# Powers on GpSimd in place of square roots and reciprocals, and forced placement of some scan products, in a two-layer image network

## The chip, the cores and the metric

The kernel runs on one core of a Trainium2 chip. The metric is the device time in microseconds (us); the time before is the median of three runs. A core has five engines, which the profile calls PE (TensorE, matmul), DVE (VectorE), ACT (ScalarE), POOL (GpSimd) and SP (SyncE, which here only issues DMAs). Each engine takes its own instructions in the order of its queue.

## The reference

Sixteen images of 48 x 48 pixels with 96 channels pass through two layers. Each layer has a convolution block with a selective scan and then a small feed-forward network, each behind a layer norm. What matters here:

```python
def _ln_c(v, eps=1e-6):              # _ln_t is the same with eps=1e-5
    m = jnp.mean(v, axis=-1, keepdims=True)
    s = jnp.var(v, axis=-1, keepdims=True)
    return (v - m) / jnp.sqrt(s + eps)
...
def step(h, inp):                    # four directions k, 192 channels d, 16 states n
    d_t, u_t, B_t, C_t = inp
    h = h * jnp.exp(d_t[..., None] * A) + (d_t * u_t)[..., None] * B_t[:, :, None, :]
    return (h, jnp.einsum('bkdn,bkn->bkd', h, C_t))
...
x = x + _L0_conv_ref(_ln_c(x), ...)
t = t + _L0_ffn_ref(_ln_t(t), ...)
x = x + _L1_conv_ref(_ln_c(x), ...)  # has a norm over 192 channels of its own, rsqrt(var + 1e-05)
t = t + _L1_ffn_ref(_ln_t(t), ...)
```

So an image has five norms, 80 in all, each with one square root per pixel. The convolution blocks also use silu, softplus and sigmoid.

## The kernel before

An image and a layer make a phase, 32 phases in all. A phase is 288 scan steps, each on tiles of 128 partitions x 768 pixels; 128 partitions are 32 channels times 4 states. `scans` (L559) writes the order of all instructions out by hand: for each step n it first lets a piece of the other work run, then issues the step.

A scan step n consists of:

- the decay a = exp(rate * d), by ScalarE into PSUM (`decays`, L611). It is issued two steps ahead, and there are two such buffers.
- the product b = (delta * u) * B, by GpSimd (`added`, L617), issued three steps ahead; there are four b buffers, and one comes free when the scan that reads it is done.
- the scan h = a * h + b along the pixels, by VectorE (`step`, L674)
- the product hc = h * C, by VectorE or by GpSimd (L678). `here` (L670) decides which: two running sums, `load["gp"]` and `load["ve"]`, hold the time booked so far for GpSimd and VectorE, and a product goes to the one that is behind. If VectorE takes it, it follows its scan at once and h stays in PSUM, in a's place. If GpSimd takes it, h goes to SBUF, and the product stands behind b of step n+3 in GpSimd's queue.
- a copy of the last column into `carry` by ScalarE (L684), where the scan goes on in the next chunk
- matmuls by TensorE that sum hc over the states (`folded`, L641)

The other work of a phase is a set of generators (`first`, `middle`, `final`, L1020 to L1047) that prepare the next phase's inputs and finish those of the last one. Each `yield` gives a weight; a phase gives out the weights evenly between its steps 6 and 276. What they book for VectorE and GpSimd with `ve` and `gp` enters the two running sums. In this work stand the operations that the change touches:

- `norm` (L334), 64 times: a mean and a centring, squares by ScalarE (L350), their sum s by VectorE (L353), `Sqrt` by ScalarE (L356), `reciprocal` by VectorE (L359), and 18 scaled activations by ScalarE (L362)
- `centred` (L893), 16 times: sums by TensorE into PSUM (L920), `Sqrt` by ScalarE (L931), `reciprocal` by VectorE (L933)
- `Silu` at L468, L492 and L774, `Softplus` at L551 and `Sigmoid` at L842, by ScalarE, which are in other tables than the scan's `Exp`

Of the kernel before, what the change touches and what calls it, by code (L numbers as in the profile page):

```python
# [13 lines left out]
F32 = mybir.dt.float32  # L14
F16 = mybir.dt.float16
F8 = mybir.dt.float8e5
AF = mybir.ActivationFunctionType
ALU = mybir.AluOpType
# [5 lines left out]
DM = 96  # L24
DI = 192
NS = 16
DR = 6
NT = L // 128
# [9 lines left out]
SPARE = 1.0  # L38
# [99 lines left out]
class Net:  # L138
    def __init__(self, ctx, tc, wpack, at, b2, ffw):
        self.tc, self.nc = tc, tc.nc  # L140
        nc = self.nc
# [31 lines left out]
            nc.vector.tensor_tensor(c, c, self.ident[n, n], ALU.add)  # L173
        self.ident16 = self.const.tile([128, 128], F16, name="ident16")
        nc.vector.tensor_copy(self.ident16, self.ident)
        self.ones16 = self.const.tile([128, 128], F16, name="ones16")
        nc.vector.memset(self.ones16, 0.0)
        nc.vector.memset(self.ones16[:1, :], 1.0)
# [84 lines left out]
            self.taps[name] = d  # L263


        self.load = {"gp": 0.0, "ve": 0.0}


        self.s = []
# [59 lines left out]
    def ve(self, us):  # L329
        self.load["ve"] += us  # L330

    def norm(self, x, eps):  # L334

        nc = self.nc
        m = self.small.tile([128, NT], F32, name="m")
        nc.vector.tensor_reduce(m, x, AX.X, ALU.add)  # L338
        nc.vector.tensor_scalar_mul(m, m, -1.0 / DM)
        self.ve(2.4)  # L340
        yield 1
        xm = self.bigt([128, NT, DM], "xm")
        for i in range(NT):
            nc.scalar.activation(xm[:, i, :], x[:, i, :], AF.Identity, bias=m[:, i : i + 1])  # L344
            if i % 3 == 2:
                yield 0.8
        sq = self.bigt([128, NT, DM], "sq")
        for i in range(2):
            at = slice(i * NT // 2, (i + 1) * NT // 2)
            nc.scalar.activation(sq[:, at], xm[:, at], AF.Square)  # L350
            yield 0.8
        s = self.small.tile([128, NT], F32, name="s")
        nc.vector.tensor_reduce(s, sq, AX.X, ALU.add)  # L353
        self.ve(2)
        yield 1
        nc.scalar.activation(s, s, AF.Sqrt, bias=self.eps[eps], scale=1.0 / DM)  # L356
        yield 1.5
        r = self.small.tile([128, NT], F32, name="r")
        nc.vector.reciprocal(r, s)  # L359
        yield 1  # L360
        for i in range(NT):
            nc.scalar.activation(xm[:, i, :], xm[:, i, :], AF.Identity, scale=r[:, i : i + 1])  # L362
            if i % 3 == 2:
                yield 0.8
        return xm
# [73 lines left out]
    def before(self, t, s, x):  # L439

        nc = self.nc
        xn = yield from self.norm(x, 1e-6)
        xt = yield from self.channels_first(xn, F32, "xt")
        nc.sync.dma_start(s["xt"], xt)
        u = [None] * 3
        cb = self.get(t + "cb")
        for name, half in (("wxa", "a"), ("wxb", "b")):
            dg = self.diagonals(t + half)
            p = self.padded(name)

            def pixels(q, o):
                if half == "a":
                    nc.scalar.copy(self.inside(p, q), img(o[:, :SUB]))
                else:
                    nc.scalar.copy(self.inside(p[:64], q), img(o[:64, :SUB]))
                    nc.scalar.copy(self.inside(p[64:], q, 0), img(o[64:, :SUB]))  # L456

            yield from self.columns(0.9 if half == "a" else 1.2, pixels, (self.get(t + name), xt))
            if half == "a":
                u[0] = self.bigt([128, L], "u0")  # L460

                def put(q, o):
                    nc.scalar.activation(
                        u[0][:, q * SUB : (q + 1) * SUB], o[:, :SUB], AF.Identity, bias=cb[:, 0:1]
                    )

                yield from self.conv(p, dg, put)
                nc.scalar.activation(u[0], u[0], AF.Silu)  # L468
                yield 2
                nc.sync.dma_start(s["u"][0], u[0])  # L470
                u[2] = self.bigt([128, L], "u2")
                for i in range(3):
                    at = slice(i * HW // 3, (i + 1) * HW // 3)
                    nc.scalar.copy(swapped(u[2])[:, at], img(u[0])[:, at])
                    yield 1
                nc.sync.dma_start(s["u"][2], u[2])
            else:
                u[1] = self.bigt([128, L], "u1")

                def put(q, o):  # L480
                    nc.scalar.activation(
                        u[1][:64, q * SUB : (q + 1) * SUB], o[:64, :SUB], AF.Identity, bias=cb[:64, 1:2]
                    )
                    nc.scalar.activation(
                        swapped(u[1][64:])[:, PQ * q : PQ * q + PQ, :],
                        img(o[64:, :SUB]),
                        AF.Identity,
                        bias=cb[64:, 1:2],
                    )

                yield from self.conv(p, dg, put, True)
                nc.scalar.activation(u[1], u[1], AF.Silu)  # L492
                yield 2
                nc.sync.dma_start(s["u"][1], u[1])


        wbc = self.get(t + "wbc").rearrange("p (j m) -> p j m", j=3)
        wdt = self.get(t + "wdt").rearrange("p (j m) -> p j m", j=3)
        dts = self.bigt([4 * DR, L], "dts")

        def put(q, o):
            nc.scalar.copy(dts[:, q * SUB : (q + 1) * SUB], o[: 4 * DR, :SUB])

        yield from self.columns(1, put, *((wdt[:, j, :], u[j]) for j in range(3)), by=1)
        rows = {}

        def put(q, o):
            c, half = divmod(q, 2)
            if half == 0:
                rows[c] = self.work.tile([128, CH], F32, name="row", tag="w3")  # L510
            nc.scalar.copy(rows[c][:, half * SUB : (half + 1) * SUB], o[:, :SUB])
            if half == 1:
                to = s["bc"].rearrange("r (c w f) -> r c w f", c=NCH, w=2)[:, c]
                nc.sync.dma_start(to, rows[c])

        yield from self.columns(1, put, *((wbc[:, j, :], u[j]) for j in range(3)), by=1)


        dtw = self.get(t + "dtw").rearrange("p (a m) -> p a m", m=128)

        def inputs(pair, j, dl):

            to = s["dd"][pair, j].rearrange("p (c w f) -> p c w f", c=NCH, w=2)
            for c in range(NCH):
                du = self.work.tile([128, CH], F32, name="du", tag="w3")
                cs = slice(c * CH, (c + 1) * CH)
                nc.gpsimd.tensor_tensor(du, dl[:, cs], u[j][:, cs], ALU.mult)  # L527
                self.gp(1.82)
                if c == 0:
                    nc.sync.dma_start(to[:, :, 0, :], dl.rearrange("p (c f) -> p c f", c=NCH))  # L530
                nc.sync.dma_start(to[:, c, 1, :], du)
                yield

        beside = iter(())
        for pair in range(2):
            for j in range(3):
                col = 3 * pair + j
                dl = self.bigt([128, L], "dl")

                def put(q, o):  # L540
                    nc.scalar.activation(  # L541
                        dl[:, q * SUB : (q + 1) * SUB],
                        o[:, :SUB],
                        AF.Identity,
                        bias=self.get(t + "dtb")[:, col : col + 1],
                    )

                for w in self.columns(1, put, (dtw[:, col, :], dts)):
                    next(beside, None)
                    yield w  # L550
                nc.scalar.activation(dl, dl, AF.Softplus)  # L551
                yield 2
                beside = inputs(pair, j, dl)
        for _ in beside:
            yield 1.3
# [3 lines left out]
    def scans(self, phases):  # L559
# [97 lines left out]
        def step(n):  # L657
# [9 lines left out]

            load = self.load
            load["gp"] = max(load["gp"], load["ve"] - 4.0)
            here = load["gp"] + 2 * 1.82 > load["ve"] + 1.81 + SPARE  # L670
            load["gp"] += 1.82 if here else 2 * 1.82
            load["ve"] += 2.76 if here else 1.81
            h = a if here else self.sw.tile([128, CH], F32, name="h")
# [87 lines left out]
    def gate(self, t, xt, ya, yb):  # L761
# [3 lines left out]
        for name, n in (("wza", 128), ("wzb", 64)):  # L765
# [5 lines left out]

            yield from self.columns(0.9, put, (self.get(t + name), xt))
        for zi in z:
            nc.scalar.activation(zi, zi, AF.Silu)  # L774
        yield 3
        for c in range(NCH):
# [7 lines left out]
    def branch(self, ya, yb, src):  # L784
# [54 lines left out]
        nc.tensor.matmul(o[:DM, :1], lhsT=self.get("se2w"), rhs=s48, start=True, stop=True)  # L839
        yield 1  # L840
        s96 = self.small.tile([DM, 1], F32, name="s96")
        nc.scalar.activation(s96, o[:DM, :1], AF.Sigmoid, bias=self.get("se2b"))  # L842
        yield 1.5
        dg = self.small.tile([DM, DM], F32, name="dg96", bufs=1)
# [48 lines left out]
    def centred(self, s):  # L893
# [34 lines left out]
                yield 0.8  # L928
        yield 0.5
        r = self.small.tile([128, NT], F32, name="rt")  # L930
        nc.scalar.activation(r, o[:, :NT], AF.Sqrt, bias=self.eps[1e-5], scale=1.0 / DI)  # L931
        yield 1.5
        nc.vector.reciprocal(r, r)  # L933
        return xt, ya, yb, r


# [229 lines left out]
```

## Time and profile before

| | us |
|---|---|
| median of three runs | 26453.4 (26446.2 to 26466.6) |
| the profiled execution | 26462.3 |
| its span | 26460.5 |
| before the first scan | 250.3 |
| behind the last scan | 216.2 |
| VectorE busy, 16253 instructions | 22569.5 |
| GpSimd busy, 13134 instructions | 22811.0 |
| ScalarE busy, 26756 instructions | 15303.0 |
| TensorE busy | 18987.9 |

A group of instructions is given by line, engine, operation, what it writes and reads, the count, and after the bar the busy time in us, the mean time of one in ns, and the idle time of the engine just ahead of them with what ended it. A row of the waits says which engine and line waited for which, the us in total, the number of times and the longest. A row of the timeline begins with the time from the start of the span and the duration, both in us.

### The profile page before, as it was taken

The page shows a single profiled execution, that of the slowest core. Times are in us where ns is not written, and L with a number is a line of the kernel's source. Part 1 is how long each engine was busy: PE and PEld are TensorE (multiplying, and loading weights), DVE is VectorE, ACT ScalarE, POOL GpSimd, SP SyncE. Part 2 cuts the span into 40 slices and gives each one's busy share as a digit, 9 for nine tenths or more (in the row PEclk, how much of TensorE's full clock was granted, in tenths as well). Part 3 has the DMA queues.
Part 4 walks back from the last instruction along what each step waited for, and adds up shares of the span by engine and source line. Part 5 has one row for each costly group of instructions (what it writes and reads, how often), then busy time and mean ns, then how long its engine had stood idle before and what let it go on. Part 6 is the DMA issues. An engine that isn't in the chain of part 4 may idle for free. (4 is left out here: it accounts for less than half of the span.)

```text
span 26460.5 us, 239663 instructions
## 1 busy us (share of the span) xinstructions
PE 18987.9 (72%) x70912; PEld 7390.0 (28%) x70912; DVE 22569.5 (85%) x16253; ACT 15303.0 (58%) x26756; POOL 22811.0 (86%) x13134
## 2 busy tenths in 40 slices
PE   6777667776677766777667776678766787667766
PEld 2223222232222222222222322223222232222322
DVE  6888888888888888888888888888888888888886
ACT  4566555666556665555655566555655556565654
POOL 6888888888888888888988888888888888998886
PEclk7777768777777777777677877777767787777776
DMA  5556556565556655565655665556665555665663
GB/s 188 216 216 221 199 213 220 217 224 207 211 212 219 222 209 206 214 221 218 220 203 205 223 221 216 202 212 219 220 222 206 204 219 218 227 220 192 220 227 140
DMA packets 1283842, 5614.99 MB, mean 212 GB/s; under 512 B 236640, under 2 KB 236640, under 8 KB 1251552
## 3 DMA queue, kind: packets, MB, share of 16 engines
q1 hardware_dynamic: 1171872, 5348.09, 55.2%
q10 hardware_dynamic: 110656, 251.56, 2.8%
q8 instruction: 558, 9.14, 0.1%
q14 instruction: 756, 6.19, 0.1%
HBM read 4707.93 MB, written 891.22 MB: 212 GB/s over the span
## 5 line engine op out<-in xcount | busy, mean ns | idle before, releaser
L617 POOL TENSOR_TENSOR b<-d,bc 128x768 f32<-128x768 f32 x9216 | 16502.3, 1815 | 834.4 <-DVE a L674 811.9
L611 ACT ACTIVATE a<-d,l_a 128x768 f32<-128x768 f32 x9216 | 8316.7, 904 | 3386.6 <-DVE hc L678 2396.8
L674 DVE TENSOR_TENSOR_SCAN a<-a,carry,b 128x768 f32<-128x768 f32 x4376 | 7927.0, 1811 | 929.5 <-ACT a L611 554.6
L641 PE MATMUL py<-hc,fold_sb 128*32 128x384 f32 x36864 | 6304.0, 639 | 2345.9 <-POOL hc L678 1519.6
L678 DVE TENSOR_TENSOR hc<-a,bc 128x768 f32<-128x768 f32 x6408 | 6137.9, 958 | 1446.6 <-PE py L641 822.1
L678 POOL TENSOR_TENSOR hc<-h,bc 128x768 f32<-128x768 f32 x2808 | 5094.7, 1814 | 1987.9 <-DVE h L674 1658.8
L674 DVE TENSOR_TENSOR_SCAN a<-a,b 128x768 f32<-128x768 f32 x2032 | 3556.1, 1750 | 773.5 <-ACT a L611 285.2
L674 DVE TENSOR_TENSOR_SCAN h<-a,carry,b 128x768 f32<-128x768 f32 x1768 | 3187.6, 1806 | 185.2 <-ACT a L611 99.7
L684 ACT COPY carry<-a 128x1 f32<-128x1 f32 x4117 | 654.2, 159 | 4302.0 <-DVE hc L678 4219.1
L641 PEld LDWEIGHTS py<-hc,fold_sb 128*32 128x32 f32 x36864 | 1196.8, 124 | 6838.1 <-issue 2346.0
L318 PE MATMUL pst<-dts,wpack_sb 24*128 24x384 f32 x2304 | 1496.4, 797 | 927.9 <-ACT dl L541 902.4
L421 PE MATMUL pst<-e,dg 128*128 128x384 f32 x5184 | 1844.0, 505 | 0.0
L674 DVE TENSOR_TENSOR_SCAN h<-a,b 128x768 f32<-128x768 f32 x1040 | 1813.5, 1745 | 28.1 <-ACT carry L684 28.1
L527 POOL TENSOR_TENSOR du<-dl,u 128x768 f32<-128x768 f32 x576 | 1042.1, 1810 | 561.4 <-DMA dd<-du 333.9
L421 PE MATMUL pst<-wxa,dg 128*128 128x384 f32 x3456 | 1211.5, 500 | 17.9 <-DMA dg<-taps_l1a 12.5
L421 PEld LDWEIGHTS pst<-e,dg 128*128 128x128 f32 x5184 | 964.8, 193 | 889.1 <-issue 281.6
L318 PE MATMUL pst<-xt,wpack_sb 96*128 96x384 f32 (+1 forms) x1536 | 780.6, 644 | 494.8 <-ACT wxb L456 255.0
L318 PEld LDWEIGHTS pst<-dts,wpack_sb 24*128 24x128 f32 x2304 | 606.0, 290 | 1836.2 <-ACT dl L541 1327.2
L629 PE MATMUL py<-first,l_skip 128*128 128x384 f32 x1152 | 691.5, 692 | 585.8 <-ACT yt L654 551.5
L318 PE MATMUL pst<-y,centre 128*128 128x384 f32 (+1 forms) x1536 | 859.4, 715 | 324.9 <-ACT y L905 163.3
L318 PE MATMUL pst<-u,wpack_sb 128*128 128x384 f32 (+1 forms) x2304 | 869.6, 525 | 233.2 <-ACT u L492 183.7
L629 PE MATMUL py<-first,ident 128*128 128x384 f32 x1152 | 719.4, 717 | 377.0 <-ACT yt L654 371.7
(162 smaller groups left out, 17810.6 us busy)
## 6 DMA issues: line engine op xcount, KB each, us to landing
bc<-bc SPq DMA_DIRECT2D x3072, 768.0 KB, 6.7
d<-dd SPq DMA_DIRECT2D x2304, 768.0 KB, 5.9
dd<-dl SPq DMA_DIRECT2D x192, 1152.0 KB, 6.5
dd<-du SPq DMA_DIRECT2D x576, 384.0 KB, 3.9
y<-yt SPq DMA_DIRECT2D x576, 384.0 KB, 2.4
u<-u SPq DMA_DIRECT2D x96, 1152.0 KB, 5.8
first<-u SPq DMA_DIRECT2D x288, 384.0 KB, 3.3
first<-y SPq DMA_DIRECT2D x288, 384.0 KB, 4.1
```

The lines of the kernel that those rows point to most:

```text
L318: nc.tensor.matmul(img(o[: w.shape[1], :SUB]), lhsT=w, rhs=y, start=(k == 0), stop=(k == len(terms) - 1))
L421: nc.tensor.matmul(img(o[:, :SUB]), lhsT=dg[:n, k, :], rhs=img(p[:n], PW)[:, PQ * q + i : PQ * q + i + PQ, j : j + HW], start=(k == 0), st ...
L527: nc.gpsimd.tensor_tensor(du, dl[:, cs], u[j][:, cs], ALU.mult)
L611: nc.scalar.activation(a, of(n)[0][:, 0, :], AF.Exp, scale=rates[t][:, pair, j, i, g : g + 1])
L617: nc.gpsimd.tensor_tensor(b, d[:, 1, :], bc[:, 0, :], ALU.mult)
L629: nc.tensor.matmul(py[:, q, :SUB], lhsT=self.skip[t][:, j, :] if pair == 0 else self.ident, rhs=firsts[group][:, q * SUB : (q + 1) * SUB], ...
L641: nc.tensor.matmul(py[32 * k : 32 * k + 32, q, :SUB], lhsT=self.fold, rhs=(hcs[n + k] if q == 0 else hcs.pop(n + k))[:, q * SUB : (q + 1) ...
L674: nc.vector.tensor_tensor_scan(way(h), way(a), way(b), start, ALU.mult, ALU.add)
L678: (nc.vector if here else nc.gpsimd).tensor_tensor(hc, h, cc, ALU.mult)
L684: nc.scalar.copy(kept["carry"][:, at : at + 1], h[:, last : last + 1])
```

## The change

Three edits:

1. `norm` and `centred` no longer use `Sqrt` and `reciprocal`. A new method `to_scale` has GpSimd multiply and add, r = s * by + eps, and then raise r to the power -0.5, with a constant tile `half` of 128 x 18 values as the exponents. In `centred`, ScalarE first copies the sums from PSUM into r. The pair books 1 us for GpSimd, and `norm` gives out one unit of weight less.
2. Ahead of each `Silu`, `Softplus` and `Sigmoid` in the generators, `load["table"]` is set to 2.
3. `here` is true for a step while `load["table"]` is over 0; each step lowers it by one. So the products of the two steps that are issued next are VectorE's. The booking of times is as it was.

```diff
+        self.half = self.const.tile([128, NT], F32, name="half")
+        nc.vector.memset(self.half, -0.5)
...
-        self.load = {"gp": 0.0, "ve": 0.0}
+        self.load = {"gp": 0.0, "ve": 0.0, "table": 0}
...
+    def to_scale(self, r, s, by, eps):
+
+        nc = self.nc
+        nc.gpsimd.tensor_scalar(r, s, by, eps, ALU.mult, ALU.add)
+        nc.gpsimd.tensor_tensor(r, r, self.half, ALU.pow)
+        self.gp(1)
...
-        nc.scalar.activation(s, s, AF.Sqrt, bias=self.eps[eps], scale=1.0 / DM)
+        r = self.small.tile([128, NT], F32, name="r")
+        self.to_scale(r, s, 1.0 / DM, eps)
         yield 1.5
-        r = self.small.tile([128, NT], F32, name="r")
-        nc.vector.reciprocal(r, s)
-        yield 1
...
+                self.load["table"] = 2
                 nc.scalar.activation(u[0], u[0], AF.Silu)
...
+                self.load["table"] = 2
                 nc.scalar.activation(dl, dl, AF.Softplus)
...
-            here = load["gp"] + 2 * 1.82 > load["ve"] + 1.81 + SPARE
+            here = load["table"] > 0 or load["gp"] + 2 * 1.82 > load["ve"] + 1.81 + SPARE
+            load["table"] -= 1
             load["gp"] += 1.82 if here else 2 * 1.82
             load["ve"] += 2.76 if here else 1.81
...
-        nc.scalar.activation(r, o[:, :NT], AF.Sqrt, bias=self.eps[1e-5], scale=1.0 / DI)
-        yield 1.5
-        nc.vector.reciprocal(r, r)
+        nc.scalar.copy(r, o[:, :NT])
+        yield 0.5
+        self.to_scale(r, r, 1.0 / DI, 1e-5)
+        yield 1
```

The line that sets `load["table"]` also stands ahead of the silu at L492, those at L774 (once for the pair) and the sigmoid at L842. In the built program the table loads are 752 before and 596 after, and VectorE's products 6408 before and 6435 after, of 9216.

More of the change, by code (lines that the diff above doesn't have):

```diff
@@ L550, in before @@
                     yield w
+                self.load["table"] = 2
                 nc.scalar.activation(dl, dl, AF.Softplus)
@@ L773, in gate @@
         for zi in z:
+            self.load["table"] = 2
             nc.scalar.activation(zi, zi, AF.Silu)
@@ L841, in branch @@
         s96 = self.small.tile([DM, 1], F32, name="s96")
+        self.load["table"] = 2
         nc.scalar.activation(s96, o[:DM, :1], AF.Sigmoid, bias=self.get("se2b"))
```

## The prediction

> **What bounds the kernel now.** I read the page's busy shares first, then its costliest groups, the groups kept apart by form, the waits, and the timeline round one square root.
>
> ```profile
> PE 18987.9 (72%) x70912; PEld 7390.0 (28%) x70912; DVE 22569.5 (85%) x16253; ACT 15303.0 (58%) x26756; POOL 22811.0 (86%) x13134
> ...
> L617 POOL TENSOR_TENSOR b<-d,bc 128x768 f32<-128x768 f32 x9216 | 16502.3, 1815 | 834.4 <-DVE a L674 811.9
> ...
> L678 DVE TENSOR_TENSOR hc<-a,bc 128x768 f32<-128x768 f32 x6408 | 6137.9, 958 | 1446.6 <-PE py L641 822.1
> L678 POOL TENSOR_TENSOR hc<-h,bc 128x768 f32<-128x768 f32 x2808 | 5094.7, 1814 | 1987.9 <-DVE h L674 1658.8
> ```
>
> VectorE and GpSimd are equally full. Each of the 9216 scan steps costs GpSimd one product b (1.815 us) and VectorE one scan (about 1.8 us); a third operation, hc, is given to VectorE (0.958, 6408 times) or to GpSimd (1.814, 2808 times). The span per step is 26460.5 / 9216 = 2.87 us, against 2.45 and 2.48 us busy. So either engine can be the bound, and moving one hc trades 0.96 us of VectorE for 1.81 us of GpSimd. If the two are to stay level, a change counts 1.81/(1.81+0.96) = 0.65 of what it does to VectorE plus 0.35 of what it does to GpSimd.
>
> ```profile
> L611 ACT ACT_TABLE_LOAD x373 | 478.6, 1283 | 6.2
> L551 ACT ACT_TABLE_LOAD x187 | 239.9, 1283 | 3.3
> L356 ACT ACT_TABLE_LOAD x63 | 80.8, 1283 | 0.4
> L931 ACT ACT_TABLE_LOAD x16 | 20.5, 1283 | 0.3
> L359 DVE RECIPROCAL r<-s 128x18 f32<-128x18 f32 x64 | 16.9, 264 | 28.3 <-ACT s L356 28.3
> L396 POOL MEMSET e<- 128x50 f32 x48 | 6.7, 140 | 2.8
> ```
>
> ScalarE loads a table whenever it leaves the exponential of the scan and again when it returns. ScalarE itself has room (58%); a load hurts only if the next decay a comes late.
>
> ```profile
> DVE a L674 <- ACT a L611: 839.8, 480, 12.9
> DVE hc L678 <- PE py L641: 822.1, 231, 14.0
> POOL hc L678 <- DVE h L674: 1658.8, 1120, 14.1
> POOL b L617 <- DVE a L674: 811.9, 548, 11.0
> ```
>
> Waiting for ScalarE's a is 840 us of VectorE's 3891 us without work. Long stalls by TensorE are as large and are not touched by the change. GpSimd mostly waits for VectorE.
>
> ```profile
> 11196.21 1.28 ACT L356 ACT_TABLE_LOAD   x1
> 11197.51 0.31 ACT L356 ACTIVATE s<-s,eps 128x18 f32<-128x18 f32 x1
> 11197.83 1.28 ACT L611 ACT_TABLE_LOAD   x1
> 11197.85 0.27 DVE L359 RECIPROCAL r<-s 128x18 f32<-128x18 f32 x1 [0.87 <-ACT s L356]
> 11198.03 1.72 DVE L674 TENSOR_TENSOR_SCAN a<-a,carry,b 128x768 f32<-128x768 f32 x1
> 11199.13 0.91 ACT L611 ACTIVATE a<-d,l_a 128x768 f32<-128x768 f32 x1
> ```
>
> VectorE stands still 0.87 us, because the reciprocal sits in its queue ahead of a scan whose operands are ready. The next a is 2.9 us late, but scans have a lead of one to two steps, so little more is lost.
>
> **Part 1, the square roots.** Eighty norms change (64 at L356/L359, 16 at L931/L933). By the built order, table loads fall from 752 to 596: 156 x 1.283 = 200 us of ScalarE. [...] Here the load starts 0.01 us after the a before it (11195.30 + 0.90) and the square root 0.02 us after the load, so no drain shows; I use 200 us. [...] The gain is on VectorE: 80 x 0.264 = 21 us of reciprocals, and the wait. From the instruction times, VectorE is idle 0.89 us on average in the two steps at the 62 square roots of L356 inside the scans and 1.20 us at 15 of L931, against about 0.14 us in two quiet steps: 62 x 0.75 + 15 x 1.06 = 62 us. VectorE gets 83 us.
>
> **Part 2, the powers.** GpSimd gets 80 pairs (multiply-add, then power, on 128x18). No power is in the trace. From below, two bare passes at the memset row: 2 x 0.14, with the wait between them some 0.4 us; a negative cost is excluded, as the work is new there. [...]
>
> Waits: the multiply-add waits for the reduction at L353, and behind it in GpSimd's queue stands the b of three steps later. That b needs the buffer of an earlier scan, which is behind the same reduction on VectorE, so this wait is covered; uncovered it would be at most the reduction, 1.95 us x 64 = 125 us on GpSimd. In the 16 centred norms GpSimd waits for a ScalarE copy and TensorE's sums: 0 to 2 us each; the reciprocal at L933 waited 11.6 us in all besides the tail, so I take 0.5 us x 16 = 8 us. The scaled activations at L362 wait for GpSimd instead of VectorE. They are issued a step or two later, and the next b, behind the power, is needed as late as the a behind them: nothing, at worst 1 us x 64. No DMA is added; with one weight unit fewer per norm what follows comes up to two steps earlier (a softplus from step 250 to 248), past no queue that was late.
>
> **Part 3, the forced products.** The two steps issued right behind a silu, softplus or sigmoid are forced to VectorE: 592 steps, of which 498 were there before, so 94 move. The late a is that of the second step after, so a product that VectorE makes in between fills time in which it would wait (2.2 us of idle in the two steps at a softplus, 5.4 at a pair of silus). Hence 94 x 0.96 = 90 us under cover. By the built order VectorE has 6435 products, 27 more, so 67 go back to GpSimd in open steps, which frees 64 us there. GpSimd's product total falls by 27 x 1.81 = 49 us, but 94 x 1.81 = 170 us leave steps in which it may have nothing else, as it can run only three steps ahead with b. From the trace, 55 softplus windows of nine steps with a GpSimd product took 27.87 us, 131 without 27.67: only 0.2 us a product. I count half the 170 as lost.
>
> **Sum.** VectorE's open work: -83 - 64 = -147 us. GpSimd: +96 + 8 - 49 + 85 = +140 us. Level: 0.65 x -147 + 0.35 x 140 = -96 + 49 = -47 us. The profiled execution took 26462.3 us (span 26460.5), 9 us over the median 26453.4; I take the difference from the median: about 26406 us. The median can't tell less than about 0.2%, 53 us, from no change.
>
> **Rivals.**
> 1. *As summed, power near 1 us* (0.4 to 1.6), and the half of 170 us lost as taken or less: -90 to -20 us, 26363 to 26433. For it: 0.87 us stalls in front of ready scans. Against: at L356 GpSimd idles only 0.16 us in nine steps, so it already sets the pace there. Chance 0.42; two thirds of it lies below -53.
> 2. *The power is dear; slower.* Only 1 us is booked, so beyond that nothing is rebalanced, and where GpSimd is saturated some 0.8 of each further microsecond reaches the end: 64 us per microsecond. From -53 at 1 us the break-even is 1.8 us and the 0.2% point 2.7 us. [...] Chance 0.34, of which 0.03 falls within 0.2%.
> 3. *The relief is hidden anyway.* The stall at L356 is slack because GpSimd paces these steps, and the moved products only turn into GpSimd's idle time: 0.65 x -21 + 0.35 x 140 is +35 us, less what the lead returns: -10 to +60, 26443 to 26513. Chance 0.12, a quarter of it slower.
> 4. *The forced products work fully* (nothing of the 170 lost, a power of 0.5 us): -100 to -130, about 26335. Chance 0.12.
>
> Range: 26330 to 26720 leaves out the lane-wise power and the far end of case 4. The likeliest case's own is 26363 to 26433. Faster by over 0.2%: 0.28 + 0.12 = 0.4; within 0.2%: 0.14 + 0.03 + 0.09 = 0.26; slower: 0.31 + 0.03 = 0.34.
>
> **What would show it.** The power's row (mean above 1.8 us: slower); no loads at the norms' lines, 596 in all; VectorE's idle in the two steps at a norm falling from 0.89 to some 0.2 us; "DVE a <- ACT a" falling, but GpSimd's wait for VectorE growing if half the 170 us is lost. Wrong would be a VectorE that idles longer for b, or scaled activations waiting long for GpSimd.

## The result and the profile after

| | before | after |
|---|---|---|
| median, us | 26460.0 (4 runs) | 26237.4 (26208.7 to 26242.7, 4 runs) |
| ratio, 95% interval | | 0.9911 [0.9894, 0.9928] |
| the profiled execution, us | 26462.3 | 26237.4 |
| its span, us | 26460.5 | 26235.7 |
| VectorE's time without work, us | 3891 | 3649 |
| GpSimd's time without work, us | 3649 | 3229 |

The kernel became 223 us faster. The forecast was 47 us, and the result lies 93 us below the low end of the range. The engine rows and the groups of the products b and hc, from the page of after:

```profile
PE 18811.1 (72%) x70912; PEld 7316.1 (28%) x70912; DVE 22586.7 (86%) x16201; ACT 15074.0 (57%) x26536; POOL 23006.8 (88%) x13267
...
L627 POOL TENSOR_TENSOR b<-d,bc 128x768 f32<-128x768 f32 x9216 | 16487.0, 1813 | 590.2 <-DVE a L685 572.5
...
L689 DVE TENSOR_TENSOR hc<-a,bc 128x768 f32<-128x768 f32 x6435 | 6164.6, 958 | 1377.5 <-PE py L651 760.2
L689 POOL TENSOR_TENSOR hc<-h,bc 128x768 f32<-128x768 f32 x2781 | 5041.5, 1813 | 1799.0 <-DVE h L685 1469.4
```

VectorE has 17 us more work than before (22586.7 against 22569.5) and GpSimd 196 us more (23006.8 against 22811.0), yet the span is 225 us shorter. So nothing was gained by taking work off the two full engines. The whole gain is waiting that went: 242 us on VectorE and 420 us on GpSimd. The waits of after say which ones fell (each row: who waited for whom, us in total, times, the longest):

```profile
POOL hc L689 <- DVE h L685: 1469.4, 928, 13.7
DVE hc L689 <- PE py L651: 760.2, 262, 13.7
DVE a L685 <- ACT a L621: 641.4, 462, 5.4
POOL b L627 <- DVE a L685: 572.5, 486, 8.6
POOL r L337 <- DVE s L362: 106.5, 10, 63.4
```

VectorE's wait for the decay has a second row, that of the scans whose product is GpSimd's: they write h instead of a. In before and in after it is

```profile
DVE h L674 <- ACT a L611: 99.7, 74, 3.1
DVE h L685 <- ACT a L621: 222.4, 114, 9.3
```

Both rows together fell from 939.5 to 863.8 us, and the longest from 12.9 to 9.3 us; VectorE's wait for TensorE fell from 822.1 to 760.2. GpSimd's two waits for VectorE fell from 2471 (1658.8 + 811.9) to 2042 us. The last row of the first list is a wait that the change adds: 106.5 us, of which 33.8 and 63.4 lie ahead of the first and behind the last scan and the rest in eight norms of 1.1 us each: covered, as assumed.

The groups of after, kept apart by form, price what was added:

```profile
L621 ACT ACT_TABLE_LOAD x296 | 379.8, 1283 | 5.2
...
L369 ACT ACTIVATE xm<-xm,r 128x96 f32<-128x96 f32 x1152 | 338.8, 360 | 112.3 <-POOL r L338 112.3
...
L338 POOL TENSOR_TENSOR r<-r,half 128x18 f32<-128x18 f32 x64 | 206.1, 3220 | 5.3
...
L338 POOL TENSOR_TENSOR rt<-rt,half 128x18 f32<-128x18 f32 x16 | 51.6, 3224 | 1.3
...
L337 POOL TENSOR_SCALAR r<-s 128x18 f32<-128x18 f32 x64 | 13.6, 213 | 108.4 <-DVE s L362 106.5
```

The table loads are 596, as built. The power takes 3.22 us, the multiply-add 0.21: 3.43 us a pair and 80 x 3.43 = 275 us in all, where 96 were assumed. The prediction's own sign said: above 1.8 us, slower. The sign was there and the kernel was faster. So its price, or something beside it, was wrong, and the experiments have to tell which.

### The profile page after: what moved, and what is told of

Same layout as the page of the kernel before. It is cut to its first block, busy times and chain, and to the rows that moved or that the text cites. A ratio compares the mean times of both kernels' runs of the same rounds, so it can differ in the third digit from the quotient of the medians.

```text
span 26235.7 us, 239464 instructions
## 1 busy us (share of the span) xinstructions
PE 18811.1 (72%) x70912; PEld 7316.1 (28%) x70912; DVE 22586.7 (86%) x16201; ACT 15074.0 (57%) x26536; POOL 23006.8 (88%) x13267
## 5 line engine op out<-in xcount | busy, mean ns | idle before, releaser
L689 DVE TENSOR_TENSOR hc<-a,bc 128x768 f32<-128x768 f32 x6435 | 6164.6, 958 | 1377.5 <-PE py L651 760.2
L689 POOL TENSOR_TENSOR hc<-h,bc 128x768 f32<-128x768 f32 x2781 | 5041.5, 1813 | 1799.0 <-DVE h L685 1469.4
```

The lines of the kernel that those rows point to most:

```text
L689: (nc.vector if here else nc.gpsimd).tensor_tensor(hc, h, cc, ALU.mult)
```

## The theories and how the experiments separate them

The change does three things to the time: it replaces **operations** at the norms (square roots, reciprocals, powers), it **forces** the products behind a table change to VectorE, and by its booking of 1 us and its missing weight unit it **shifts** the rule of balance, so that from the first norm on the products of all steps fall to VectorE and GpSimd in another pattern, and the other work by up to two steps elsewhere. Only 27 products more are VectorE's, but 3465 of the 9216 are made by the other engine than in before. The prediction counted the first two and took the third as an even trade. Theory 1: the first two are worth far more than assumed. Rival: the shift by itself, which does no work, is worth most. Later rivals concern why a shift is worth anything: fewer products on GpSimd, one held DMA issue, or products of particular steps.

Each experiment was measured in five rounds beside before on the same chip; differences below are to that median of before (26450.1, 26458.0, 26461.2, 26468.4 and 26465.6 us in the five groups; for after, 26460.0 from the section on the result). VectorE's products and the long stalls come from the profiled execution of each kernel; the long stalls are VectorE's idle time in all those steps, from one scan's start to the next, that have over 3 us of it. Most of what a kernel gains shows there, but not all (e2, e5).

| kernel | median | difference, us | ratio, 95% | products of VectorE | long stalls, us |
|---|---|---|---|---|---|
| before | | 0 | | 6408 | 1483 |
| after | 26237.4 | -223 | 0.9911 [0.9894, 0.9928] | 6435 | 1187 |
| powers and shift (e1) | 26318.1 | -132 | 0.9949 [0.9935, 0.9962] | 6435 | 1255 |
| forced only (e2) | 26380.0 | -70 | 0.9969 [0.9958, 0.9981] | 6408 | 1495 |
| shift only (e3) | 26296.7 | -153 | 0.9938 [0.9925, 0.9950] | 6435 | 1275 |
| after, cheap power (e4) | 26173.8 | -276 | 0.9893 [0.9880, 0.9907] | 6435 | 1190 |
| booking only (e5) | 26308.4 | -150 | 0.9949 [0.9936, 0.9961] | 6435 | 1410 |
| weight only (e6) | 26321.0 | -137 | 0.9949 [0.9936, 0.9961] | 6407 | 1273 |
| start one step later (e7) | 26430.4 | -28 | 0.9988 [0.9981, 0.9994] | 6407 | 1418 |
| another threshold (e8) | 26284.8 | -173 | 0.9938 [0.9925, 0.9950] | 6412 | 1283 |
| issue moved in before (e9) | 26413.3 | -48 | 0.9982 [0.9975, 0.9989] | 6408 | 1460 |
| in after (e10) | 26185.8 | -275 | 0.9891 [0.9878, 0.9905] | 6435 | 1157 |
| in e8 (e11) | 26243.5 | -218 | 0.9912 [0.9898, 0.9925] | 6412 | 1224 |
| in e5 (e12) | 26256.2 | -205 | 0.9920 [0.9906, 0.9933] | 6435 | 1379 |
| one step's stall out of before (e13) | 26453.1 | -15 | 0.9994 [0.9985, 1.0003] | 6408 | 1414 |
| put into e8 (e14) | 26328.1 | -140 | 0.9951 [0.9939, 0.9964] | 6412 | 1356 |
| rule in before (e15) | 26167.3 | -301 | 0.9888 [0.9875, 0.9902] | 6408 | 1236 |
| rule and issue in after (e16) | 26099.1 | -369 | 0.9868 [0.9853, 0.9883] | 6435 | 1027 |
| rule in after (e17) | 26182.5 | -283 | 0.9895 [0.9882, 0.9909] | 6435 | 1114 |
| another residue in before (e18) | 26477.0 | +11 | 1.0003 [0.9994, 1.0012] | 6408 | 1506 |

## Experiments: the parts one by one

**e1, powers without the forced products.** After, with the override taken out:

```diff
-            here = load["table"] > 0 or load["gp"] + 2 * 1.82 > load["ve"] + 1.81 + SPARE
+            here = load["gp"] + 2 * 1.82 > load["ve"] + 1.81 + SPARE
```

> The powers on GpSimd as in the changed kernel, without the forced products. Theory A (the relief at the norms carries the gain: no table loads, no reciprocal in front of ready scans): 150 to 220 us faster than before, 26240 to 26310. Theory B (the forced products carry it, because they fill the waits behind a change of table): within 50 us of before, or slower, since each pair on GpSimd takes 3.4 us. Theory C (neither; products and other work merely stand elsewhere and meet the long stalls differently): no sure size, but the same as the run with the schedule alone.

Measured: -132 us. From e1 to after, the override is worth -81 us by the two medians, -91 by the two differences to before.

**e2, the forced products alone.** Before, with `load["table"] = 2` ahead of each silu, softplus and sigmoid, and

```diff
-            here = load["gp"] + 2 * 1.82 > load["ve"] + 1.81 + SPARE
+            here = load["table"] > 0 or load["gp"] + 2 * 1.82 > load["ve"] + 1.81 + SPARE
+            load["table"] -= 1
```

> The forced products alone; square roots and reciprocals as before. Theory A: 0 to 50 us faster than before. Theory B: 150 us faster or more, 26250 to 26310. Theory C: no sure size.

Measured: -70 us, near the -81 from the other side. VectorE has 6408 products as in before (93 went to it, 93 went back), so the gain isn't in how many move but in which.

**e3, the shift alone.** Before, with its square roots and reciprocals, and only the booking and the weights of after:

```diff
         nc.vector.reciprocal(r, s)
-        yield 1
+        self.gp(1)
...
-        yield 1.5
+        yield 0.5
         nc.vector.reciprocal(r, r)
+        self.gp(1)
+        yield 1
```

> Square roots by ScalarE and reciprocals by VectorE as before; only the changed kernel's booking of 1 us for GpSimd at each norm and its weights between the pieces of other work. Theories A and B: within 30 us of before, 26430 to 26490. Theory C: 100 to 220 us faster, as the changed kernel.

Measured: -153 us, for a kernel with the same work as before, in which 3429 products are on the other engine than in before (27 more on VectorE, net). This decides the first question. The new operations come on top of it: from e3 to e1 the time goes up by 21 us (the two intervals overlap, so the sign isn't certain). Shift -153, operations +21, override -81: -213, near the -223 of the whole.

**e4, a power at the price of a multiplication.** After, with the scales of the norms not computed:

```diff
-        nc.gpsimd.tensor_tensor(r, r, self.half, ALU.pow)
+        nc.gpsimd.tensor_tensor(r, r, self.half, ALU.mult)
```

> The changed kernel with a multiplication by -0.5 in place of the power, so the norms' scales are not computed. The power took 3.22 us, a multiplication of this size some 0.2. If GpSimd's time at the norms reaches the end as the prediction had it (0.8 of each microsecond): 80 x 3 x 0.8 = 190 us faster than the changed kernel, 26045. If it is covered: 0 to 40 us faster.

Its group shows what the power cost:

```profile
L338 POOL TENSOR_TENSOR r<-r,half 128x18 f32<-128x18 f32 x64 | 14.4, 225 | 5.3
```

3220 - 225 = 3.0 us less in each of 80 pairs is 240 us of GpSimd. The time fell by 64 us (53 by the differences to before): 0.22 to 0.27 us of the end for each microsecond. Every product is on the same engine as in after, so this is a clean price. The prediction's rule of level loads gave 0.35, its second rival 0.8.

## Experiments: what in the shift does it

**e5, the booking alone**: before, with `self.gp(1)` at each norm.

```diff
         nc.vector.reciprocal(r, s)
+        self.gp(1)
         yield 1
```

> The kernel before with 1 us more booked for GpSimd at each of the 80 norms, nothing else; VectorE then has 6435 products instead of 6408. Theory S1 (GpSimd had too many products; 27 fewer are worth the 153 us that the run with the schedule alone gained): 100 to 150 us faster than before. Theory S2 (the weights carry it): within 30 us of before. Theory S3 (any small shift of the order moves the time by this much, for better or worse, and before stood badly): anything from 0 to 150 us faster, and the placebos below move too.

Measured: -150 us.

**e6, the weight alone**: before, without the last `yield 1` of `norm`, and with 0.5 and 1 in `centred`.

```diff
         nc.vector.reciprocal(r, s)
-        yield 1
```

> The kernel before with one unit of weight less at each norm of 64, so that what follows stands about one step earlier per norm; booking as before. S1: within 30 us of before. S2: 100 to 150 us faster. S3: anything from 0 to 150 us faster.

Measured: -137 us, and VectorE has 6407 products, one fewer than in before. So the net 27 products that the booking moves are not what is gained.

**e7 and e8, two changes that mean nothing**: the other work starts one step later, or the threshold of the balance is lower.

```diff
-START, END = 6, 276
+START, END = 7, 277
```

> A placebo: the kernel before with all other work one scan step later (7 to 277 instead of 6 to 276), same work, 6407 products by VectorE. S1 and S2: within 30 us of before. S3: 50 us or more from before, in either direction, faster more likely.

```diff
-SPARE = 1.0
+SPARE = 0.0
```

> A second placebo: the kernel before with the threshold between the running sums at 0 instead of 1 us, which changes which steps give their product to GpSimd but hardly how many (6412 by VectorE). S1 and S2: within 30 us of before. S3: 50 us or more from before in either direction.

Measured: -28 and -173 us. A threshold that changes the count of VectorE's products by 4, but puts 3806 of the 9216 on the other engine, is worth more than the booking, and more than the -70 us or so that the operations and the override bring without the shift. So the order in before was an unlucky one, and three of these four edits leave it.

Where is the gain? By the starts of the scans, the 32 phases fall into four kinds, by their index modulo 4. The mean duration of a phase of each kind, in us, eight phases each:

| kernel | kind 0 | kind 1 | kind 2 | kind 3 |
|---|---|---|---|---|
| before | 797.0 | 838.9 | 815.7 | 797.5 |
| e3 | 799.1 | 817.0 | 813.4 | 800.0 |
| e5 | 798.0 | 820.9 | 816.0 | 795.5 |
| e6 | 796.9 | 822.6 | 815.1 | 797.1 |
| e7 | 796.7 | 827.9 | 826.1 | 798.8 |
| e8 | 797.3 | 822.5 | 813.5 | 793.3 |
| e2 | 794.8 | 837.8 | 813.7 | 792.7 |
| after | 790.0 | 819.9 | 814.3 | 795.9 |

In the phases of kind 1, in which the scan of the first layer runs beside `middle` (the convolution of another image's first layer), before is 16 to 22 us longer than e3, e5, e6, e8 and after: 8 x 19 = 152 us, the size of the shift's gain. The other kinds stay within 4.2 us of before in these, except kind 0 in after (-7.0). e7 shortens kind 1 by 11 us and makes kind 2 10 us longer. In e2 kind 1 keeps its length, and the gain is in small amounts elsewhere.

What VectorE waited for in these eight phases, in us, all eight together:

| kernel | all its idle time | for the decay | for a fold (TensorE) | for the carry | the rest |
|---|---|---|---|---|---|
| before | 1054 | 390 | 224 | 147 | 293 |
| e3 | 880 | 277 | 195 | 168 | 241 |
| e5 | 911 | 265 | 230 | 152 | 264 |
| e6 | 929 | 312 | 203 | 171 | 242 |
| e8 | 908 | 338 | 175 | 145 | 252 |
| after | 903 | 297 | 197 | 172 | 237 |

So the larger part of what went in e3, e5, e6 and after is waiting for ScalarE's decay; in e8 the decay and the folds lost some 50 us each. In e5, which gains 150 us, the wait for the folds did not fall at all, in the whole kernel either (822.1 in before):

```profile
DVE hc L679 <- PE py L642: 827.3, 264, 12.5
```

Which products bring the decays earlier was not tried by itself. The stall that is easiest to follow is one at a fold.

One stretch of such a phase shows it. VectorE in before (start, duration, engine, line, operation; in brackets the idle time before it and who ended it):

```profile
11057.70 1.82 DVE L674 TENSOR_TENSOR_SCAN h<-a,carry,b 128x768 f32<-128x768 f32 x1 [3.85 <-ACT carry L684]
11059.43 1.80 DVE L674 TENSOR_TENSOR_SCAN a<-a,carry,b 128x768 f32<-128x768 f32 x1
11061.33 0.96 DVE L678 TENSOR_TENSOR hc<-a,bc 128x768 f32<-128x768 f32 x1
11062.21 1.81 DVE L674 TENSOR_TENSOR_SCAN a<-a,carry,b 128x768 f32<-128x768 f32 x1
11073.86 0.96 DVE L678 TENSOR_TENSOR hc<-a,bc 128x768 f32<-128x768 f32 x1 [9.84 <-PE py L641]
```

The last product's scan is done, and it still stands 9.84 us: there are eight `hc` buffers, and the one it needs comes free when TensorE has folded the four steps that it belongs to (L641). TensorE in before, the same stretch:

```profile
11059.27 6.38 PE L318 MATMUL pst<-y,wpack_sb 128*128 128x384 f32 x8 [7.29 <-ACT e L795]
11065.58 1.65 PE L629 MATMUL py<-first,l_skip 128*128 128x384 f32 x2
11067.15 1.51 PE L641 MATMUL py<-hc,fold_sb 128*32 128x384 f32 x8
11068.59 3.62 PE L318 MATMUL pst<-y,wpack_sb 128*128 128x384 f32 x8
11072.15 0.91 PE L629 MATMUL py<-first,l_skip 128*128 128x384 f32 x2
11072.99 0.85 PE L641 MATMUL py<-hc,fold_sb 128*32 128x384 f32 x8
```

The fold at 11072.99 ends the stall: it is over at 11073.84, and the product starts at 11073.86. It stands behind two blocks of the other work (L318, 6.38 and 3.62 us), the first of which had itself waited 7.29 us for ScalarE. Why it stands behind them is in the code (lines of before):

```python
            kept["last"] = max(kept["last"], n + (1 if here else 3))            # L686
            if n % 4 == 3:
                at = max(n + 1, kept["last"])
                folds.extend([(at, n - 3, 0), (at + 1, n - 3, 1)])
```

A product that GpSimd makes takes 1.81 us, behind a product b of the same length in its queue; one that VectorE makes takes 0.96 us, behind its scan. The first is finished later, so the program puts its fold later: for the last step of a group of four, at n + 3 and n + 4 instead of n + 1 and n + 2 (if the two products ahead of it are VectorE's). In two steps, blocks of other matmuls get ahead of it in TensorE's queue. In before, step 83 of the phase (83 = 4 x 20 + 3, the last of its group) is GpSimd's in all eight phases of kind 1, and step 88, five later, takes 12.3 to 16.7 us instead of 2.8. In e8 step 83 is VectorE's. VectorE in e8, the same steps:

```profile
10965.03 1.80 DVE L674 TENSOR_TENSOR_SCAN a<-a,carry,b 128x768 f32<-128x768 f32 x1
10966.92 0.96 DVE L678 TENSOR_TENSOR hc<-a,bc 128x768 f32<-128x768 f32 x1
10967.79 1.81 DVE L674 TENSOR_TENSOR_SCAN a<-a,carry,b 128x768 f32<-128x768 f32 x1
10969.71 0.96 DVE L678 TENSOR_TENSOR hc<-a,bc 128x768 f32<-128x768 f32 x1
10970.97 1.82 DVE L674 TENSOR_TENSOR_SCAN h<-a,carry,b 128x768 f32<-128x768 f32 x1 [0.30 <-ACT carry L684]
```

No stall. e6 is mixed, and so a test inside one kernel: its phases with step 83 on GpSimd have 12.3 to 12.7 us at step 88, the others 2.8 or 2.9. In e3, e5 and after three of the eight phases have step 83 on GpSimd; their step 88 takes only 3.9 us, but over steps 84 to 91 VectorE is idle for 12 to 17 us in them, in the other five for 2.3 to 2.8. e7, whose other work comes one step later, goes against it: its one phase with step 83 on GpSimd has 3.5 us of idle time there, and five of the seven with step 83 on VectorE have 12 to 13. So it is the placement together with where the other work lies. And the sum is not this one stall: from before to e3, e5 or after the 86 us of waiting for a fold at step 88 are gone in all eight phases, but new waits for folds stand at steps 8, 89 and 92. Three of four runs of three steps give two products to VectorE and one to GpSimd, and a phase has 288 steps, divisible by three; this fits a pattern that falls the same way in each phase of a kind.

## Experiments: the held DMA issue, a rival

The 7.29 us that TensorE waited in that stretch had a striking source. ScalarE in before:

```profile
11048.57 0.41 ACTq L1017 DMA_DIRECT2D xs<-in_x_dram  x1
...
11049.01 7.45 ACTq L405 DMA_DIRECT2D dg<-taps_e  x1
...
11056.50 0.16 ACT L684 COPY carry<-a 128x1 f32<-128x1 f32 x1 [6.57 <-issue]
```

ScalarE issues a load of 2304 packets of 384 bytes (L1017), and the next issue on its queue, the taps (L405), holds it for 7.45 us; the carries, decays and e behind it are late. The same issue takes 0.33 us in most of its 48 instances. Over 3 us it takes in 8 of before, 3 of after, 4 of e5 and 2 of e8, all of them right behind that load; the other 8 that stand behind it in before take 2.0 to 2.7 us. So the rival is that the shift only changes how often an issue is held. e9 to e12 place the load right behind the taps, in before, after, e8 and e5:

```diff
             dg = self.diagonals(f"e{m}")
+            if m == 2:
+                x = self.tokens(src)
...
-            if m == 1:
-                x = self.tokens(src)
```

> The kernel before, with the load of the image's tokens (2304 packets of 384 bytes) issued just behind the load of the last tap matrices on ScalarE's queue instead of just ahead of it. In before, eight of those tap loads hold ScalarE for 7 to 9 us. Theory D (these held issues, and TensorE and the products behind them, are why before is slow and what the other placements avoid): 100 to 160 us faster than before, 26300 to 26360. Theory C (no single place; any shift of the order does it): within 50 us of before, or no sure sign.

> The same exchange of the two loads in the changed kernel, where three tap loads are held that long. Theory D: 20 to 70 us faster than the changed kernel, 26170 to 26215. Theory C: no sure sign.

> The same exchange with the threshold of the running sums at 0, which alone made before 173 us faster. Theory D: within 40 us of the exchange in before, since the placement of the products then has nothing left to avoid. Theory C: as far from it as without the exchange, 100 us or more.

> The same exchange with 1 us more booked for GpSimd at each norm, which alone made before 150 us faster. Theory D: within 40 us of the exchange in before. Theory C: 100 us or more from it.

Measured: -48 us in before, -52 to after, -41 to e8, -52 to e5. No issue of the taps is over 3 us any more. This order of the two loads costs something near 50 us in each of the placements, and the distance between the placements stays (from e9 to e11 it is 170 us). This rival, theory D, falls: the order of the loads is a cost of its own, not what the change removed.

## Experiments: products of single steps

**e13 takes the stall out of before**, by exchanging steps 83 and 84 in phases of kind 1, with the booking left as it was:

```diff
             load["ve"] += 2.76 if here else 1.81
+            if f % 4 == 1 and n % STEPS in (83, 84):
+                here = n % STEPS == 83
```

> The kernel before, with the product of step 83 made by VectorE and that of step 84 by GpSimd in the eight phases where it was the other way round; booking and all other placements untouched. Theory E (a product on GpSimd in the last step of a fold group that opens a new sum delays that sum's matmuls by two steps, behind other TensorE work, and VectorE then waits for a free product buffer; over all traces a GpSimd product at step 83 goes with 9.4 us more idle behind it): 8 x 9 = 75 us faster than before, 26365 to 26410, and step 88 without its 10 us. Theory C (no single place): within 25 us of before.

**e14 puts it into e8**, with `here = n % STEPS == 84` in the same place.

> The converse: the run with the threshold at 0 (26285), with step 83's product given to GpSimd and step 84's to VectorE in those eight phases. Theory E: 75 us slower than that run, 26340 to 26380. Theory C: within 25 us of it.

e14 behaved as the theory says: step 88 went from 2.8 to 12.5 to 17.0 us in all eight phases, those phases grew by 8.8 us each (8 x 8.8 = 70), and the kernel by 43 us against e8 (33 by the differences to before, 84 in the profiled executions). VectorE in e14:

```profile
11013.07 1.80 DVE L676 TENSOR_TENSOR_SCAN a<-a,carry,b 128x768 f32<-128x768 f32 x1
11028.26 0.96 DVE L680 TENSOR_TENSOR hc<-a,bc 128x768 f32<-128x768 f32 x1 [13.40 <-PE py L641]
```

e13 did not: it gained 15 us where 75 were expected, and its interval reaches no change. Step 88 fell from 13.4 to 5.2 us on average, but step 89 rose from 1.7 to 6.2. VectorE in e13, the scans of steps 88 and 89:

```profile
11054.57 1.82 DVE L676 TENSOR_TENSOR_SCAN h<-a,carry,b 128x768 f32<-128x768 f32 x1 [2.37 <-ACT a L611]
11060.75 1.82 DVE L676 TENSOR_TENSOR_SCAN a<-a,carry,b 128x768 f32<-128x768 f32 x1 [4.36 <-ACT carry L686]
```

The wait for the fold is gone, and waits for ScalarE stand in its place. Over the phases of kind 1 the wait for folds fell by 61 us, as the theory says, and those for the carry and the decay rose by 47 and 12: the phases take 838.5 us as before (838.9). So one placement can make a stall of 10 us (e14), but taking the stall out did not shorten the phase (e13), and step 88 alone isn't what makes kind 1 long in before.

**e15 to e18: a rule for many steps.** Sixteen steps make one sum py, and the steps with n mod 16 = 3 are the last of the group of four that opens a sum. Over all traces up to e14, the idle time of VectorE in the six steps behind a step is 0.9 us larger on average when a step with n mod 16 = 3 is GpSimd's than when it is VectorE's; for the other residues it is between 1.2 less and 0.4 more. The residues 7, 11 and 15 are last of a group of four too and show next to nothing (0.2, 0.0 and -0.6), so the two steps of delay alone don't make the cost; why it takes the group that opens a sum wasn't tried. If a deferred fold of that group is a cost, a rule that keeps residue 3 on VectorE gains, and the same rule on a residue that isn't the last of a group of four (9 = 4 x 2 + 1) doesn't:

```diff
-            here = load["gp"] + 2 * 1.82 > load["ve"] + 1.81 + SPARE
+            here = n % 16 == 3 or load["gp"] + 2 * 1.82 > load["ve"] + 1.81 + SPARE
```

> The kernel before with every sixteenth step's product (the fourth step of each sum, n mod 16 = 3) always VectorE's, the running sums keeping the balance. Theory E in all places: 100 to 200 us faster than before, 26250 to 26360. Theory C: no sure size.

e16 has the same term in after, with the load moved as in e10; e17 in after alone; e18 is e15 with `n % 16 == 9`.

> The changed kernel with the exchange of the two loads (26186) and the same rule for every sixteenth step. Theory E: 20 to 80 us faster than with the exchange alone, 26105 to 26165. Theory C: within 40 us of it, either way.

> The changed kernel with every sixteenth step's product (n mod 16 = 3) VectorE's. Theory E (most of the change's gain was a better placement by chance): close to before with the same rule (26167), 26120 to 26170, so the change is then worth under 50 us. If instead the change's gain is its own: 200 us under it, about 25965.

> A placebo of the rule: in the kernel before, the products with n mod 16 = 9 (208 of them on GpSimd, against 154 with n mod 16 = 3) are always VectorE's. Theory E: at most the gain of the other chance placements, 0 to 150 us faster than before, 26310 or more. Theory C (any regular rule does it): 250 to 300 us faster, 26165 to 26215.

Measured: the rule gains 301 us in before, with none of the change's operations and VectorE's 6408 products as they were in number. The control residue gains nothing (+11 us, interval across no change). The waits of e15:

```profile
DVE a L674 <- ACT a L611: 835.6, 461, 13.5
...
DVE hc L678 <- PE py L641: 355.8, 149, 11.5
```

and of e18:

```profile
DVE hc L678 <- PE py L641: 810.6, 261, 14.0
```

The wait for the fold is 355.8 us where before had 822.1, and the control left it at 810.6. VectorE's idle time in the steps with n mod 16 = 8 and 9, five and six behind the rule's, fell by 238 us together, of 299 in all steps. The wait for the decay stayed (959.0 us with the row for h, before 939.5), and that for the carry rose by some 140. All four kinds of phases got shorter, by 11.1, 11.6, 6.9 and 7.3 us. So deferred folds of the groups that open a sum are a cost that the kernel before pays, and a bare rule about which engine makes a product collects more than the whole change. No rule on the residues 7, 11 or 15 was run.

In after the rule gains only 55 us (e17), although its wait for TensorE falls as well; its waits for the decay and the carry rose by 92 and 95 us:

```profile
DVE hc L689 <- PE py L651: 468.9, 175, 11.2
```

With the rule in both, after is no faster than before: 26182.5 against 26167.3. With the load moved too (e16), 26099.1 us is the shortest time of all.

## Why the prediction was wrong

Its direction was right and its size was not. Point by point:

- **What bounds the kernel.** Two equally full engines: right. The row "DVE hc <- PE py", 822 us, was put aside as "not touched by the change". The change moves products, and the engine of a product sets when its fold is issued, so it was touched: the 86 us at step 88 of the phases of kind 1 went, others came, and the row fell no further than to 760. The wait for the decay was read as 840 us; with the scans that write h it was 940.
- **The failed step** is in part 2: "with one weight unit fewer per norm what follows comes up to two steps earlier [...], past no queue that was late", charged at nothing, together with the count of the 27 moved products as a plain exchange between two engines. The runs show -153 us for this (e3), by the booking alone -150 (e5), by the weight alone -137 (e6). Waits for late queues did go: in the phases of kind 1 the wait for ScalarE's decay fell by 78 to 126 us in these three, the wait for TensorE's folds by at most 30. Which of the 3429 products that changed engine in e3 do it stays open. Without the shift the change is worth about -223 + 153 = -70 us, where the forecast said -47.
- **The price of the power** was mis-sized. The 96 us that the sum has for the powers are 1.2 us for each of 80 pairs; that was the author's estimate, and no run shows it. The runs show 3.43 us for a pair (3.22 for the power, 0.21 for the multiply-add): 179 us more on GpSimd. What a microsecond of it costs was mis-sized in the other direction: at most 0.27 us of the end (e4) instead of the second rival's 0.8. By that rival's line a pair of 3.43 us would give -53 + 64 x 2.43 = +103 us for the whole change; without its shift it comes to about -70.
- **The norms.** The relief came as forecast and was given back. VectorE's idle time in the two steps at a norm fell from 0.89 to 0.20 us. But over nine steps a norm takes 22.59 us in before and 22.52 in after, with VectorE idle for 1.39 and 1.40. After's timeline at a norm shows why:

```profile
13407.60 1.80 DVE L685 TENSOR_TENSOR_SCAN a<-a,carry,b 128x768 f32<-128x768 f32 x1
...
13409.49 0.96 DVE L689 TENSOR_TENSOR hc<-a,bc 128x768 f32<-128x768 f32 x1
13409.59 0.22 POOL L337 TENSOR_SCALAR r<-s 128x18 f32<-128x18 f32 x1
13409.90 3.22 POOL L338 TENSOR_TENSOR r<-r,half 128x18 f32<-128x18 f32 x1
13410.36 1.81 DVE L685 TENSOR_TENSOR_SCAN h<-a,carry,b 128x768 f32<-128x768 f32 x1
...
13413.07 3.57 POOL L627 TENSOR_TENSOR b<-d,bc 128x768 f32<-128x768 f32 x2
13413.15 0.90 ACT L369 ACTIVATE xm<-xm,r 128x96 f32<-128x96 f32 x3 [1.57 <-POOL r L338]
```

  VectorE goes from product to scan without a gap, but on GpSimd the two products b follow the power at once, without a gap either: it sets the pace, and the power is a delay that VectorE meets a few steps later. With the cheap power the nine steps take 21.77 us, 0.75 less than in after, and 62 x 0.75 = 46 of e4's 53 to 64 us. So the third rival had the mechanism at the norms right, and gave it 0.12. The scaled activations waited 112.3 us for GpSimd in 62 places, at ScalarE, at most 5.6 us; this was to be a sign of a wrong forecast, and no row shows it reaching the end.
- **The forced products** work as argued, with the size too small: by the prediction's rule they were 0.65 x -64 + 0.35 x 36 = -29 us; measured are -70 (e2) and -81 (e1 to after). The windows of nine steps behind a table change are of that size: from before to e2 a softplus window falls from 28.21 to 27.89 us, a single silu's from 25.40 to 25.10, a pair's from 29.14 to 28.64; times 186, 62 and 31 windows that is 94 us. From e1 to after the same sum is 61. Begun a step earlier or later, the windows give some 80 to 165 and some 60 to 100 us, so they show the size and not the sum. VectorE's wait for the decay fell by 97 us in all, from 939.5 to these two rows of e2:

```profile
DVE a L678 <- ACT a L614: 640.6, 363, 12.3
DVE h L678 <- ACT a L614: 201.7, 137, 3.8
```

  The half of 170 us that was counted as lost on GpSimd was to show as a longer wait for VectorE; that wait fell, in e2 from 2471 to 2367 us.

That the operations and the override come to -70 where -47 was forecast is luck in part: the power was taken as too cheap and the override as worth too little, and a microsecond on GpSimd, counted at 0.35, costs 0.22 to 0.27. The direction, too, hung on the placement: with the rule of e15 in both kernels, the change is worth nothing.

**What stays open.** The gain of the rule differs by 246 us between before and after (301 and 55), and e13 got back 15 of some 75 us. Placement effects don't add, and how far times spread over many equally valid placements under one rule wasn't measured; 28 to 173 us were seen for four shifts (e5 to e8). So how much of the override's 70 to 91 us is the table change, and how much its own shift, isn't settled beyond the windows above, and the 15 us between e15 and e17 can't be told from chance. Why ScalarE's decays came earlier in the phases of kind 1, which is the larger part of the shift's gain, was not followed; only the stall at step 88 was, and taking it out of before (e13) did not shorten them.

## What to carry to other kernels

When two engines are about equally full (85% and 86% of the span here) and work stands behind what was issued ahead of it on the same engine (here a fold behind blocks of 6.38 and 3.62 us), a small edit to a balance or a weight can re-deal which engine does which step: four such edits gained 28 to 173 us here (e5 to e8). So before crediting an edit with its result, run it beside edits that do nothing (another threshold, another start), and against the kernel with only its bookings. Ask of every product that can go to either engine which buffer it holds and whose queue its consumer is put into: here two steps of delay in TensorE's queue cost VectorE ten microseconds (e14). Then look at the whole stretch and not at the one stall: in e13 waits for ScalarE took its place (47 us for the carry and 12 for the decay, against 61 for folds). At the norms, relief on VectorE was not kept (nine steps took 22.59 and 22.52 us), because GpSimd set the pace there; relief on GpSimd was in part (e4: 53 to 64 of 240 us).

## What was not expected of the hardware

- A power of 128 x 18 values on GpSimd takes 3.22 us, a multiplication of the same shape 0.225 us.
- A DMA issue on ScalarE's queue right behind one of 2304 packets of 384 bytes held ScalarE for 7.45 us in the instance shown (up to 8.6), where 0.33 us is usual; placing the long one behind it was worth 41 to 52 us in four kernels. Behind the same load it took 2.0 to 2.7 us in other phases. What in the queue holds it wasn't tried by itself.
